# Two graph layers on one core: three dense chunks instead of four, list work at other places, dense R gathered straight to its place

## Chip, cores and metric

The kernel runs on one core of a Trainium2 chip. The metric is the device time in microseconds (us), the median of several runs. Where the profile is read, times are those of one profiled execution.

## What is computed

There are 8 batches of 2048 nodes with 128 features, x[b, n, f], and one matrix adj (2048 x 2048) with about 9 non-zero entries in a row. All data are float32. Layer 0 and layer 1, in short:

```python
sj, si = x @ g_w[:128], x @ g_w[128:256]
res = si[:, :, None] + sj[:, None, :] + adj[None] * g_w[256] + g_b
agg = jnp.einsum('bij,bjd->bid', res, x)
x = layernorm(x + agg @ weight + bias)

x1 = jnp.einsum('bnf,nw->bwf', x, adj)               # hop, order 1
x2 = 2 * jnp.einsum('bnf,nw->bwf', x1, adj) - x      # hop, order 2
xs = concat([x, x1, x2, x1, x2])                     # the same adj twice
x = layernorm(x + relu(xs @ Theta1 + bias1))
```

In layer 0 the product with adj is sparse, and what remains of `res` has low rank: for each half of the batch it is a product of five columns (four of si and one of ones) with five rows (column sums, and the row of sums weighted by sj and g_b with the bias). Both halves together are the "rank-9 part". In layer 1 the five thetas are merged to three: u = x1 th0, y = A'u + x1 th1 (hop 1) and out = layernorm(x1 + relu(A'y + x1 th2 + b)) (hop 2), A' the transposed adj.

## The kernel before

**Tiles.** The nodes are 16 chunks of 128 rows. A row of a chunk holds all 8 batches, 1024 numbers (4 KB), so a chunk's tile is 128 x 1024 (512 KB) and its product fills two PSUM banks. All matmuls are float32.

**Phase A** (loop over R_ORDER, line 328) loads adj row chunk by row chunk (1 MB each), transposes it on PE (row_groups, 244; ACT copies it out and scales it by wr) and stores the transposed columns of most chunks to DRAM (store_rt, 264), where rr_d[c] later holds, for each node, the entries of both directions. SP issues these loads and stores in the order of the list `todo` (pump, 216). Every second step takes a tile of x with it: transposes (x_t, 267) and y0 = x @ weight (y_of, 277). DVE takes block maxima (mask_rows, mask_columns): which rows of 32 columns have a non-zero entry.

**Phase B** (the X loop, 688) does the other eight tiles of x, with the dense product of chunks 0 and 1 (full_rows, 311) after each, and building steps of the lists between (lists_at, 667).

**Lists.** Chunks 4 to 15 do not multiply with all of adj. For each chunk there are seven lists of up to 128 rows: four T lists (32 columns each), two H lists of 64 columns and one of 128 columns. DVE finds the rows with rounds of eight largest numbers (round_of, 463; rounds2, 658), and lists_end (468) turns them into indices (idx, idr). For each list a job gathers the entries of adj from rr_d into staging (get_job, 533, four buffers `st`), and DVE copies them, masked, to `rct` for layer 0 and `rc` for layer 1 (keep_job, 546). Then for each list and each of the three products a gather fetches 128 rows of y0, u or y from DRAM (get_rows, 714), and PE multiplies them (listed, 722). A gather is an indirect DMA that POOL issues, one instruction for a list. Twelve tiles of Y take gathered rows in turn.

**Dense chunks** 0 to 3 are full products in layer 0 only, of 16 blocks x 2 halves of 128 x 512; chunks 2 and 3 run after phase B (777 to 836), between the list jobs. In layer 1 they use lists as well; their entries are gathered from adj into a tile `trp` (28 gathers of 128 x 128) and kept by DVE in `rc`.

**List loop** (839 to 862), chunks 4 to 15 in layer 0: rows and jobs, own block (own_rows, 765), rank9 (614), which needs a small transpose (si_t, 607), the lists, z_add, make_u (647), layernorm (628). x for the sum is loaded by load_z (213) two chunks ahead into ring tiles; own rows of y0 for chunks from 8 on and the own block of adj come by load_own (755) on SP.

**Hops** (865 to 929, called at 931 and 937): for each chunk theta rows (8 matmuls), own rows, T lists, H lists, and `end`. Hop 1 stores y, hop 2 adds x1, takes the layernorm of the chunk and stores 512 KB of output from ACT's queue. The order of chunks is 4 to 13, 0 to 3, 14, 15 in hop 1, and 9 to 13, 0 to 3, 14, 15, 4 to 8 in hop 2; T lists only use rows of the first 14 chunks, so they can start before the last chunks are done.

**What sets the order.** A wrapper (Tied, 66 to 72) keeps each engine's instructions in the order in which the program issues them, in the places near the change. Therefore almost all instructions carry line 72 in the profile, and are told apart by their tiles. Numbers in names of buffers are left out there: `Y<-y_d` stands for gathers from y0_d in layer 0 and from y_d in hop 2. A gather on POOL that waits holds every gather behind it.

Of the kernel before, what the change touches and what calls it, by code (L numbers as in the profile page):

```python
# [18 lines left out]
def kernel(  # L19
# [30 lines left out]
    ND = 4  # L50
# [5 lines left out]
    PAD = 40000  # L56
    W = 3 * P
    T_ORDER = list(range(6, NC)) + [4, 5]
# [3 lines left out]
    X_ORDER = list(range(ND, NC)) + list(range(ND))  # L62
# [27 lines left out]
    rct = keep.tile([P, NS * W], F32, name="rct")  # L90
# [24 lines left out]
    def load_constants():  # L115
        with nc.allow_non_contiguous_dma(reason="two columns of 128 numbers"):
            act.dma_start(out=wx[:, D:D + 2], in_=g_w[0:2 * D].rearrange("(t p) -> p t", p=P))
        act.dma_start(out=wx[:, 0:D], in_=weight)
        act.dma_start(out=wr, in_=g_w[2 * D:2 * D + 1][None, :].to_broadcast([P, 1]))
        act.dma_start(out=gb, in_=g_b[None, :].to_broadcast([P, 1]))  # L120
        for i in range(4):
            act.dma_start(out=b0row[:, i, :], in_=bias0[None, :])
        act.dma_start(out=b1bc[:, 0, :], in_=bias1[None, :].to_broadcast([P, D]))
        act.dma_start(out=th, in_=theta.rearrange("(m p) f -> p m f", p=P))

    ctx.enter_context(nc.allow_non_contiguous_dma(reason="512-byte rows of a block of 128 columns"))
    load_constants()
# [4 lines left out]
    e5 = const.tile([1, 5], F32)  # L132
    dve.memset(e5, 0.0)
    dve.memset(e5[:, 4:5], 1.0)
# [4 lines left out]
    sel5 = const.tile([P, 4, 5], F32)  # L139
    dve.memset(sel5, 0.0)  # L140
    for i in range(4):
        dve.tensor_copy(sel5[:, i, i:i + 1], sel[:, 0:1])
        dve.tensor_copy(sel5[:, i, 4:5], sel[:, 1 + i:2 + i])
# [3 lines left out]
    dve.tensor_copy(num, numi)  # L147
    coli = const.tile([P, NI], I32)
    pool.iota(coli[:, 0:NT], pattern=[[1, NC], [0, QT]], base=0, channel_multiplier=0)
    pool.iota(coli[:, NT:NT + 2 * NC], pattern=[[1, NC], [0, 2]], base=0, channel_multiplier=0)  # L150
# [12 lines left out]
    si = const.tile([P, NC, 37], F32)  # L163
    dve.memset(si, 0.0)
    for h in range(2):
        dve.memset(si[:, :, 32 * h + 4:32 * h + 5], 1.0)
# [16 lines left out]
    ats += [Y[:, n:n + 2].rearrange("p c b f -> p (c b f)") for n in X_ORDER[NX::2]]  # L183

    def at_of(c):
        t = at4[:, c] if c < ND else ats[(c - ND) % len(ats)]
        return t.rearrange("p (j i) -> p j i", i=P)
# [13 lines left out]
    todo += [("x", 8), ("s", 12), ("x", 9), ("s", 13), ("x", 10), ("x", 11), ("s", 14), ("x", 12)]  # L201
    todo += [("s", 15), ("x", 13), ("x", 14), ("x", 15)] + [("c", c) for c in T_ORDER]
# [10 lines left out]
    def load_z(c):  # L213
        zs[c] = load_x(c, [ring[:, 3], ring[:, 4], ring[:, 5], spare][(c - 2) % 4])

    def pump():
        while todo:
            what, n = todo[0]
            if what == "a" and n < done["a"] + 3:
                sp.dma_start(out=am[n % 3], in_=adj[R_ORDER[n] * P:(R_ORDER[n] + 1) * P, :])  # L220
            elif what == "x" and n < done["x"] + 6:
                c = X_ORDER[n]
                xin[c] = load_x(c, ring[:, X_SLOT[n % 6]])
                if c < ND:
                    zs[c] = xin[c]
            elif what == "s" and done["a"] == NC:
                store_rt(n)
            elif what == "c" and done["a"] == NC:
                copies([n])
            else:  # L230
                return
            todo.pop(0)
# [52 lines left out]
    def s_rows(c0):  # L285
# [5 lines left out]
        for h in range(2):  # L291
            act.copy(si[:, c4, 32 * h:32 * h + 4], sraw[:, c4, h * HB:(h + 1) * HB, 1])
# [15 lines left out]
    LAST = list(range(ND)) + list(range(8, NC)) + list(range(4, 8))  # L308
# [18 lines left out]
    pump()  # L327
    for k, n in enumerate(R_ORDER):
# [139 lines left out]
    def lists_end(part):  # L468
# [17 lines left out]
        s = slice(lo, hi)  # L486
        rown = small.tile([P, NT], F32, name=f"rown{part}", tag="rown")[:, 0:hi - lo]
# [4 lines left out]
        dve.scalar_tensor_tensor(rown, rown, float(NC), col[:, s], op0=ALU.mult, op1=ALU.add)  # L492
# [14 lines left out]
    adj128 = adj.rearrange("n (c f) -> (n c) f", f=P)  # L507
# [15 lines left out]

    jobs = [("T", c) for c in T_ORDER] + [("H", c) for c in range(ND, NC)]
    for c in range(ND):
        jobs += [("T", c), ("H", c)]
    got, kept = [0], [0]
    last = trp[:, 2].rearrange("p i f -> p (i f)")

    def staged(k):  # L530
        return st[:, k % 4 * BD:] if jobs[k][1] >= ND else last

    def get_job():
# [3 lines left out]
        for n, i in enumerate(columns(c, what)):  # L537
            if c >= ND:
                gather(
                    s[:, n * 2 * P:(n + 1) * 2 * P], rr_d[c - ND].rearrange("n m f -> n (m f)"), idx,  # L540
                    i, N,
                )
            else:
                gather(s[:, n * P:(n + 1) * P], adj128, idr, i, N * NC)

    def keep_job():
# [3 lines left out]
        m = 2 if c >= ND else 1  # L550
        hc = has[:, columns(c, what)[0]:columns(c, what)[0] + QT]
        for k in range(m):
            if m == 1 or k == 1:
                to = rc[:, c * W:(c + 1) * W]
            else:
                to = rct[:, (c - ND) * W:(c - ND + 1) * W]
            of = s[:, k * P:]
            if what == "T":
                if m == 2:
                    dve.tensor_mul(  # L560
                        to[:, 0:P].rearrange("p (t f) -> p t f", t=QT),
                        strided(of, QT, m * P + TW, TW), hc[:, :, None].to_broadcast([P, QT, TW]),
                    )
                    continue
                for t in range(QT):
                    at = t * (P + TW)
                    dve.tensor_scalar(
                        to[:, TW * t:TW * t + TW], of[:, at:at + TW], hc[:, t:t + 1], None,
                        op0=ALU.mult,
                    )  # L570
                continue
            step = m * P + 64
            dve.tensor_mul(
                to[:, P:2 * P].rearrange("p (t f) -> p t f", t=2), strided(of, 2, step, 64),
                hc[:, 0:2, None].to_broadcast([P, 2, 64]),
            )
            i = NT + 2 * NC + c
            dve.tensor_scalar(
                to[:, 2 * P:3 * P], of[:, 2 * m * P:2 * m * P + P], has[:, i:i + 1], None,
                op0=ALU.mult,  # L580
            )

    def make_ub():
# [4 lines left out]
        for h in range(2):  # L588
            pe.matmul(
                pu[32 * h:32 * h + 5], e5, b0row.rearrange("p i f -> p (i f)"), start=True,  # L590
                stop=False, skip_group_check=True, tile_position=(0, 32 * h),
            )
        for i in range(4):
            s = slice(i * P, (i + 1) * P)
            for h in range(2):
                pe.matmul(
                    pu[32 * h:32 * h + 5, s], sel5[:, i, :], cs[h][:, s], start=False, stop=(i == 3),
# [9 lines left out]
    def si_t(c):  # L607
        b = bank[turns[turn[0] % len(turns)]][0:37, 0:P]
        turn[0] += 1
        pe.transpose(b, si[:, c, :], ident)  # L610
        sits[c] = small.tile([37, P], F32, name=f"sit{c}", tag="sit")
        act.copy(sits[c], b)

    def rank9(c, accs):
        sit = sits.pop(c)
        for h in range(2):
            pe.matmul(
                accs[h], sit[32 * h:32 * h + 5], ub[32 * h:32 * h + 5].rearrange("p i f -> p (i f)"),
                start=False, stop=(c < ND), skip_group_check=True, tile_position=(32 * h, 0),
# [47 lines left out]
    def lists_at(n):  # L667
        if n == 9:
            ranked()
        if n == 10:  # L670
# [3 lines left out]
            dve.tensor_reduce(miss[:, 1:2], both, AX.XY, ALU.add)  # L674
            thetas()
        if n == 13:
# [3 lines left out]
            encode2()  # L680
            get_job()
            get_job()
        if n == 14:
            split2()
        if n == 15:
            candidates2()

    for n in range(NX, NC):
        xt = x_t(n)
        pump()  # L690
        y_of(n, xt)
        lists_at(n)
        for c, acc in enumerate((acc0, acc1)):
            full_rows(c, acc, [X_ORDER[n - 1]])
# [12 lines left out]
    load_z(4)  # L707

    NG = 12
    G = [flat(Y[:, n]) for n in LAST[:NG]]  # L710
    g_at = [0]
    rows_of = {}

    def get_rows(i, c, what, src):
        hi = LT if what == "T" else NC
        for n, q in enumerate(columns(c, what)):
            g = G[g_at[0] % NG]
            g_at[0] += 1
# [3 lines left out]
    def listed(i, c, accs, what):  # L722

        r = rc[:, c * W:(c + 1) * W] if i else rct[:, (c - ND) * W:(c - ND + 1) * W]
# [26 lines left out]
    homes = [seven[(c + 8) % 12 % 7] for c in range(12)] + [slab(k) for k in range(4)]  # L751
# [21 lines left out]
    def own0(c):  # L773
        load_own(0, y0_d, c, Y[:, c] if c < 8 else ring[:, c % 2], c < 8)


    rounds2([0])
# [3 lines left out]
    rounds2([1, 2])  # L781
# [4 lines left out]
    load_z(ND + 1)  # L786
    rounds2([3, 4])
# [4 lines left out]
    rank9(1, acc1)  # L792
    rounds2([5, 6])
    next_job()
    rounds2([7])
    lists_end(1)
# [4 lines left out]

    acc2 = bank[4:6]
    full_rows(2, acc2, LAST[:5])
    next_job()
    next_job()
    make_u(0, zs[0], x1t[0], u_of[0], 0)
    layernorm(zs[1], "0_1")
    full_rows(2, acc2, LAST[5:11])
    next_job()
    make_u(1, zs[1], x1t[1], u_of[1], 0)  # L810
    next_job()
    full_rows(2, acc2, LAST[11:])
    si_t(2)
    rank9(2, acc2)
    z_add(acc2, zs[2])
    overflow()
    next_job()
    layernorm(zs[2], "0_2")

    acc3 = bank[2:4]  # L820
    full_rows(3, acc3, LAST[:8])
    next_job()
    next_job()
    get_rows(0, ND, "T", y0_d)
    get_rows(0, ND, "H", y0_d)
    own0(ND)
    own0(ND + 1)
    full_rows(3, acc3, LAST[8:])
    keep_job()
    keep_job()  # L830
    get_rows(0, ND + 1, "T", y0_d)
    si_t(3)
    rank9(3, acc3)
    si_t(ND)
    z_add(acc3, zs[3])
    layernorm(zs[3], "0_3")


    for c in range(ND, NC):
        if c > ND:  # L840
            if c > ND + 1:
                get_rows(0, c, "T", y0_d)
            get_rows(0, c, "H", y0_d)
        if c < 15:
            keep_job()
        if c < 13 or c == 14:
            get_job()
        accs = acc_pair()
        own_rows(0, c, accs, True)
        if c + 2 < NC:  # L850
            own0(c + 2)
        rank9(c, accs)
        if c + 1 < NC:
            si_t(c + 1)
        listed(0, c, accs, "T")
        listed(0, c, accs, "H")
        z_add(accs, zs[c])
# [177 lines left out]
```

## Time and profile before

| | us |
|---|---|
| median of 3 runs (lowest, highest) | 810.49 (807.04, 811.39) |
| the profiled execution | 818.08 |
| its span | 816.3 |
| PE matmul busy | 732.8 (90%), 3554 instructions |
| DVE busy | 394.7 (48%) |
| POOL busy | 445.2 (55%), 432 instructions |
| ACT busy | 192.7 (24%) |
| DMA | 253.90 MB, mean 311 GB/s |
| mean granted clock | 0.971 of full speed |

Busy time is that of the engine's records; POOL's are mostly gathers, and a record of a gather is its issue on POOL, not the transfer. "Idle before" names what ended a wait; "issue" is time in which the engine waited for nothing that the profile shows. DMA share is the busy share of the core's 16 DMA engines.

The chain of work that ended last is 52% PE, 29% DMA and 6% issue. By transfer, 12% is `Y<-u_d` (gathers in hop 1) and 8% `Y<-y_d`.

### The profile page before, as it was taken

Reading aid. Unit: us, or ns where it says so; the run is one execution under the profiler, and the core shown is the slowest. Engines: PE = TensorE matmul, PEld = TensorE weight load, DVE = VectorE, ACT = ScalarE, POOL = GpSimd, SP = SyncE. Lnnn points to the kernel's source line nnn. Section 1 sums busy time; section 2 is a strip of 40 time slices with the busy share of each in tenths; the row PEclk is TensorE's granted clock in tenths of the full one; section 3 lists DMA queues with packets and bytes.
Section 4 is the critical chain, followed back from the end, with each engine's and each line's share of the span. In section 5 each row is a group of like instructions: output and inputs, shape, how many; then the busy total and the mean of one; then the engine's idle time right before and its main releaser. Section 6 shows DMA issues by size and latency. Waiting matters only on the chain.

```text
span 816.3 us, 10067 instructions
## 1 busy us (share of the span) xinstructions
PE 732.8 (90%) x3554; PEld 364.9 (45%) x3554; DVE 394.7 (48%) x591; ACT 192.7 (24%) x439; POOL 445.2 (55%) x432
## 2 busy tenths in 40 slices
PE   4999999997999998988798888898899999999992
PEld 4666566642644343434345243333344454444441
DVE  4664876578341655555533000000100377777775
ACT  3757554321200332313222000000000011111101
POOL 1000000477747876776344677776774777776740
PEclk9999999997999999999899899999999999999997
DMA  8999999999326799999969799899999799999982
GB/s 264 296 314 316 352 292 295 314 398 347 119 89 223 244 346 368 341 344 367 356 224 344 246 364 360 314 365 346 339 372 357 252 343 357 370 385 389 363 299 68
DMA packets 165299, 253.90 MB, mean 311 GB/s; under 512 B 17255, under 2 KB 118020, under 8 KB 163192
## 3 DMA queue, kind: packets, MB, share of 16 engines
q0 software_dynamic: 49280, 146.52, 49.7%
q1 hardware_dynamic: 93200, 81.01, 31.1%
q10 hardware_dynamic: 22760, 25.63, 8.9%
q8 instruction: 30, 0.49, 0.2%
q14 instruction: 29, 0.24, 0.1%
HBM read 234.82 MB, written 58.72 MB: 360 GB/s over the span
## 4 chain that ended last, share of the span: by engine, by line
PE 52%; DMA 29%; issue 6%; ACT 6%; DVE 3%; POOL 2%; ACTq 0%; POOLq 0%; SPq 0%; DVEq 0%
PE bank L72 52%; DMA Y<-u_d,idx 12%; DMA Y<-y_d,idx 8%; DMA st<-rr_d,idx 2%; DMA rd<-rr_d 2%; ACT Y L72 2%; DMA ring<-in_x_dram 2%; POOL Y L72 1%; ACT rct L72 1%; ACT trp L72 1%; DMA trp<-in_adj_dram,idr 1%; DVE s L72 1%; DVE ring L72 1%; ACT at L72 1%; DVE st L72 1%
## 5 line engine op out<-in xcount | busy, mean ns | idle before, releaser
L72 POOL DMA_INDIRECT Y<-y_d,idx x196 | 212.0, 1081 | 93.2 <-PE bank L72 38.0
L72 PE MATMUL bank<-Y,rc 128*32 128x512 f32 (+2 forms) x896 | 219.7, 618 | 21.3 <-DMA Y<-u_d,idx 19.1
L72 POOL DMA_INDIRECT st<-rr_d,idx x84 | 90.3, 1075 | 183.5 <-DVE rown L72 148.3
L72 POOL DMA_INDIRECT Y<-u_d,idx x112 | 111.8, 999 | 53.9 <-issue 29.9
L72 PEld LDWEIGHTS bank<-Y,rc 128*32 128x32 f32 (+2 forms) x896 | 58.6, 130 | 179.3 <-issue 99.5
L72 PE MATMUL bank<-Y,at 128*128 128x512 f32 x256 | 115.2, 601 | 0.0
L72 PE MATMUL bank<-Y,rct 128*32 128x512 f32 (+2 forms) x336 | 77.3, 625 | 8.5 <-DMA Y<-y_d,idx 8.5
L72 DVE TENSOR_REDUCE s<-sq 128x4 f32<-128x512 f32 x64 | 43.9, 686 | 58.0 <-ACT sq L72 58.0
L72 PEld LDWEIGHTS bank<-Y,at 128*128 128x128 f32 x256 | 47.8, 193 | 53.6 <-issue 53.4
L72 DVE COPY ring<-bank 128x512 f32<-128x512 f32 x10 | 6.9, 692 | 110.1 <-PE bank L72 110.1
L72 ACT ACTIVATE sq<-ring 128x512 f32<-128x512 f32 x44 | 27.7, 630 | 129.5 <-DVE ring L72 109.7
L72 PE MATMUL bank<-ring,rd 128*128 128x512 f32 x108 | 51.5, 599 | 5.7 <-DMA rd<-rr_d 4.1
L72 PE MATMUL bank<-ident,rc 128*128 128x128 f32 (+2 forms) x302 | 45.0, 297 | 12.6 <-DMA rc<-in_adj_dram 6.6
L72 PE MATMUL bank<-th,at 128*128 128x128 f32 x384 | 49.2, 283 | 1.9 <-ACT at L72 1.9
L72 PEld LDWEIGHTS bank<-th,at 128*128 128x128 f32 x384 | 46.8, 197 | 6.7 <-ACT at L72 3.8
L72 DVE TENSOR_TENSOR ring<-bank,ring 128x512 f32<-128x512 f32 x26 | 17.3, 688 | 66.0 <-PE bank L72 60.8
L72 DVE TENSOR_REDUCE st<-rc 128x64 f32<-128x2048 f32 x16 | 36.5, 2283 | 25.7 <-DMA rc<-in_adj_dram 25.7
L72 ACT COPY ring<-bank 128x512 f32<-128x512 f32 x34 | 19.9, 586 | 122.5 <-PE bank L72 112.9
L72 PEld LDWEIGHTS bank<-Y,rct 128*32 128x32 f32 (+2 forms) x336 | 20.8, 130 | 57.3 <-issue 32.4
L72 PEld LDWEIGHTS bank<-ident,rc 128*128 128x128 f32 (+2 forms) x302 | 33.8, 150 | 25.5 <-issue 9.1
L72 PE MATMUL bank<-wx,trp 128*128 128x130 f32 x256 | 36.9, 288 | 4.3 <-ACT trp L72 2.2
L72 PE MATMUL bank<-ident,ring 128*128 128x128 f32 x232 | 32.5, 282 | 6.4 <-DMA ring<-in_x_dram 2.8
(142 smaller groups left out, 789.1 us busy)
## 6 DMA issues: line engine op xcount, KB each, us to landing
rc<-in_adj_dram SPq DMA_DIRECT2D x16, 1024.0 KB, 10.9
ring<-in_x_dram SPq DMA_DIRECT2D x25, 512.0 KB, 8.5
rr_d<-in_adj_dram SPq DMA_DIRECT2D x12, 1024.0 KB, 10.8
rr_d<-Y SPq DMA_DIRECT2D x8, 1024.0 KB, 9.0
y_d<-Y SPq DMA_DIRECT2D x16, 512.0 KB, 10.6
u_d<-ring ACTq DMA_DIRECT2D x12, 512.0 KB, 7.0
ring<-y_d SPq DMA_DIRECT2D x11, 512.0 KB, 23.2
ring<-u_d SPq DMA_DIRECT2D x10, 512.0 KB, 3.9
```

What stands on the lines that cost most here:

```text
L72: return lambda *a, **k: tc.keep_in_program_order(f(*a, **k))
```

## The change

1. ND is 3: chunk 3 is no longer dense. It has lists, a stored transpose (store_rt) and a column copy like chunks 4 to 15. Its entries for layer 0 lie in a corner of `at4`.
2. Steps of lists_at run at three places in a step of x: ahead of y_of, after it, and between the two dense chunks' matmuls. The candidates, lists_end(0), the first four jobs, split2 and candidates2 come at earlier places, and the first three rounds of the second lists run within the x loop.
3. Entries of chunks 0 to 2 for layer 1 are gathered straight into `rc` by 21 indirect DMAs of 128 x 32, 64 or 128 (get_direct), after POOL has set that part of rc to zero. The 28 gathers into trp and their keeps are gone. 17 of the 21 are issued in the list loop, four in hop 1.
4. For list chunks the rank-9 part becomes nine rows in the third H list: rows 119 to 127 of its row tile hold u (ub_rows writes them once into two fixed tiles, C0), and si is written into the entries of the same rows (si_rows, 13 small matmuls). rank9 and si_t remain for the dense chunks. Each H job has one more DVE operation on rows 96 to 127, an addition.
5. Gathered rows use different tiles: in layer 0 ten in turn (seven of Y, ring 0 and 1, Y 3) and two (C0) for the third H list; in the hops twelve of Y. Own rows of y0 stay in Y for chunks 3 to 11. z is loaded into x1t[c], up to four chunks ahead.
6. At the start, adj rows come in two loads of 512 KB, wr is the first constant, and six later constants move to SP's list behind the 16 adj chunks and the first tiles of x.
7. Hop 1 begins three chunks (T lists, theta and own rows) before its loop instead of two, the third in banks 4 and 5, and its order starts at chunk 3. In hop 2 the last two chunks are computed by halves of the batch: by_halves does the matmuls of one half, then its sum, layernorm and a 256 KB store, the end of a half being issued after the beginning of the next.

The core of the diff (constants, tables for rank 9 and indices of columns left out):

```diff
-    ND = 4
+    ND = 3
...
-    ats += [Y[:, n:n + 2].rearrange("p c b f -> p (c b f)") for n in X_ORDER[NX::2]]
+    ats += [at4[:, 3]] + [Y[:, n:n + 2].rearrange("p c b f -> p (c b f)") for n in X_ORDER[NX::2]]
...
     def load_z(c):
-        zs[c] = load_x(c, [ring[:, 3], ring[:, 4], ring[:, 5], spare][(c - 2) % 4])
+        zs[c] = load_x(c, x1t[c])
...
-                sp.dma_start(out=am[n % 3], in_=adj[R_ORDER[n] * P:(R_ORDER[n] + 1) * P, :])
+                for w in (slice(0, N // 2), slice(N // 2, N)):
+                    sp.dma_start(
+                        out=am[n % 3][:, w], in_=adj[R_ORDER[n] * P:(R_ORDER[n] + 1) * P, w]
+                    )
...
+    def get_direct(n):
+        for at, w, i in direct[:n]:
+            gather(
+                rc[:, at:at + w], adj.rearrange("n (c f) -> (n c) f", f=w), idr, i, N * (N // w)
+            )
+        del direct[:n]
...
+    def si_rows(c0, n):
+
+        b = by4(bank[turns[turn[0] % len(turns)]])[LC:]
+        turn[0] += 1
+        for i in range(n):
+            pe.matmul(
+                b[:, i, :], si[:, c0 + i, :], ident, start=True, stop=True, skip_group_check=True,
+                tile_position=(0, LC),
+            )
...
     for n in range(NX, NC):
         xt = x_t(n)
         pump()
+        lists_at(n, 0)
         y_of(n, xt)
-        lists_at(n)
-        for c, acc in enumerate((acc0, acc1)):
-            full_rows(c, acc, [X_ORDER[n - 1]])
+        lists_at(n, 1)
+        full_rows(0, acc0, [X_ORDER[n - 1]])
+        lists_at(n, 2)
+        full_rows(1, acc1, [X_ORDER[n - 1]])
+        if n == 14:
+            rounds2([0])
+        if n == 15:
+            rounds2([1, 2])
...
-    NG = 12
-    G = [flat(Y[:, n]) for n in LAST[:NG]]
-    g_at = [0]
+
+
+    G0 = [flat(Y[:, n]) for n in LAST[:7]] + [flat(ring[:, 0]), flat(ring[:, 1]), flat(Y[:, 3])]
+    C0 = [flat(ring[:, 5]), flat(spare)]
+    G1 = [flat(Y[:, n]) for n in list(range(4)) + list(range(8, NC))]
...
     for c in range(ND, NC):
-        if c > ND:
-            if c > ND + 1:
-                get_rows(0, c, "T", y0_d)
+        if c > 4:
+            get_rows(0, c, "T", y0_d)
+        if c > 3:
             get_rows(0, c, "H", y0_d)
-        if c < 15:
-            keep_job()
-        if c < 13 or c == 14:
-            get_job()
-        accs = acc_pair()
-        own_rows(0, c, accs, True)
+        k, g = (2, 2) if c < 5 else (2 if c in (7, 8) else 1 if c < 15 else 0, 1 if c < 13 else 0)
+        for n in range(max(k, g)):
+            if n < k:
+                keep_job()
+            if n < g:
+                get_job()
+        get_direct(0 if c < 8 else 1 if c < 13 else 3)
+        if c == 3:
+            accs = acc3
+        else:
+            accs = acc_pair()
+            own_rows(0, c, accs, True)
         if c + 2 < NC:
             own0(c + 2)
-        rank9(c, accs)
-        if c + 1 < NC:
-            si_t(c + 1)
         listed(0, c, accs, "T")
         listed(0, c, accs, "H")
...
         for k, c in enumerate(order):
+            if i == 2 and k >= NC - 2:
+                rows(k, "H")
+                rows(k + 1 if k + 1 < NC else NC, "T")
+                by_halves(k)
+                continue
             rows(k, "H")
-            if k > 1:
+            if k >= begun:
                 begin(k)
-            fetch(k + 2)
-            if k > 0:
+            if k + 2 >= begun:
+                fetch(k + 2)
+            if k + 1 >= begun:
                 rows(k + 1, "T")
-            if i == 1 and (k % 2 and k < 12 or k == 12):
-                keep_job()
-                if k < 12:
-                    get_job()
+            if i == 1:
+                get_direct(1)
             listed(i, c, accs[k], "H")
             end(c, accs[k])
```

In by_halves, a half of a chunk runs as follows (its matmuls, from the transposes to list H, write one bank only):

```python
                zh, sq = begun_half(homes[c], accs[h], b, h, s)
                if halves:
                    ended_half(*halves.pop())
                halves.append((c, zh, sq, h, s))
            if k == NC - 1:
                ended_half(*halves.pop())
```

## The prediction, made before the result was known

> **What bounds the kernel now.** I read the span in stretches first: one row a stretch, with its length, the busy time of PE, PEld, DVE, ACT and POOL (instructions in brackets), the clock, the DMA share and GB/s.
>
> ```profile
> 0.00:109.50 109.50, 91.22 (x504) 63.23 (x505) 69.03 (x60) 64.10 (x145) 2.82 (x12) 1.00 0.98 307
> 109.50:173.90 64.40, 61.59 (x325) 39.81 (x326) 42.21 (x75) 26.66 (x97) 17.33 (x17) 1.00 1.05 316
> 173.90:262.10 88.20, 80.49 (x288) 36.47 (x288) 43.09 (x85) 13.72 (x26) 62.04 (x59) 0.92 0.62 213
> 262.10:429.50 167.40, 149.76 (x734) 67.05 (x735) 91.29 (x153) 47.79 (x96) 108.50 (x106) 0.98 0.92 324
> 429.50:451.70 22.20, 16.81 (x121) 10.86 (x119) 6.11 (x8) 6.06 (x11) 11.01 (x11) 0.99 0.91 326
> 451.70:625.20 173.50, 158.70 (x697) 63.94 (x698) 13.87 (x35) 9.38 (x16) 125.52 (x127) 0.95 0.95 345
> 625.20:641.40 16.20, 14.35 (x81) 6.43 (x79) 0.69 (x1) 0.00 (x0) 6.26 (x7) 1.00 0.64 228
> 641.40:801.40 160.00, 159.90 (x817) 77.12 (x816) 121.00 (x167) 23.41 (x45) 111.70 (x98) 1.00 0.96 344
> 801.40:816.30 14.90, 0.00 (x0) 0.00 (x0) 7.39 (x10) 1.56 (x3) 0.00 (x0) 0.66 0.24 73
> ```
>
> I call them A (adj turned), B (rest of x), C (dense chunks), D (list chunks of layer 0), E (turn), F (hop 1), G (turn), H (hop 2), I (tail). PE is busy 90% and looks like the bound. It is in C and H. In A and B the DMA engines are full. POOL's 55% hides the rest: its timeline (start, length, idle before it) shows that a gather busy for 1.0 us is always followed by 0.3 us that no wait explains.
>
> ```profile
> 223.66 1.00 POOL L72 DMA_INDIRECT st<-rr_d,idx  x1 [0.30 <-issue]
> 224.96 0.99 POOL L72 DMA_INDIRECT st<-rr_d,idx  x1 [0.30 <-issue]
> 234.74 1.00 POOL L72 DMA_INDIRECT st<-rr_d,idx  x1 [8.79 <-DVE rc L72]
> 399.08 0.99 POOL L72 DMA_INDIRECT Y<-y_d,idx  x1 [0.30 <-issue]
> 410.68 0.99 POOL L72 DMA_INDIRECT Y<-y_d,idx  x1 [10.61 <-PE bank L72]
> ```
>
> So a gather costs 1.30 us of POOL. With its small stretches I measure, start to start, 1.36 over the 55 from 151.7 to 225.0 and 1.365 over the 129 from 447.4 to 622.2. That last run is stage F: 129 x 1.365 = 176 us. F is POOL's queue, and the DMA engines (0.95) are close behind. In D the pitch is 1.33 to 1.42, plus stalls of 8.8, 4.5 and 10.6 us; the one at 399 is PE late, because a transfer of own entries (rd) took 19.4 us. The groups of POOL in F give the mean length of each kind:
>
> ```profile
> L72 POOL DMA_INDIRECT Y<-u_d,idx x99 | 98.0, 990 | 35.3 <-issue 21.2 <-PE bank L72 8.0 <-DMA Y<-u_d,idx 6.0
> L72 POOL DMA_INDIRECT trp<-in_adj_dram,idr x20 | 20.0, 999 | 9.4 <-issue 4.9 <-DVE rc L72 3.3 <-DMA Y<-u_d,idx 1.3
> ```
>
> A gather of 64 KB (trp) costs POOL what one of 512 KB (Y) does. Last, two stretches in which DMA is the limit, 371 to 394 GB/s:
>
> ```profile
> 590.00:622.00 32.00, 30.65 (x148) 13.08 (x149) 2.08 (x3) 1.76 (x3) 23.16 (x24) 0.95 1.00 380
> 720.00:740.00 20.00, 20.00 (x105) 9.73 (x104) 15.90 (x22) 2.97 (x6) 15.53 (x15) 1.00 1.03 394
> ```
>
> **The change part by part.**
>
> *A and B.* The first x tile now is not behind late constants: PE waited for it until 16.5, and I take 4.5 us off (2.5 to 6.5). But DMA is full (share 1.05), and chunk 3 by lists adds a 1 MB store (3.2 us at 316 GB/s) and a column copy (3.45 us each in SP's rows). Sixteen more load issues and six constants pass SP in A, where SP waits for room anyway: nothing, or +1 if a load is late. The stores of y0, queued behind it all on SP, landed at 193; I take 195 (191 to 198). The row gathers wait for them. The list steps moved between pairs of x bring the first lists some 7 us earlier (lists_end(0) at 150 before) and the second's rounds (DVE, 167.6 to 191.2) some 11. Those DVE steps were beside full DMA and PE; what could show is PE behind them in its queue, +0 to 2.
>
> *C and D.* Off PE: dense chunk 3, 27.6 us (the trace has two records of 0.43 for each of 16 x 2 matmuls), and rank9 with si_t, 1.06 + 0.23 for 12 chunks, 15.5. On PE: a listed chunk, 7.4 with its own rows, the few ub_rows and si_rows, about 4. Off DVE: the 24 keep operations of dense chunks, most of them in F. On DVE: one more small operation (0.28) for each H job, hidden, as DVE is busy 91 of 167 in D. PE thus loses 32 us in C and D, if PE bounded them.
>
> POOL does not lose. Its order in the new program has 32 gathers of adj entries before the first row gather of layer 0. From that one to the last row gather of layer 0 stand 91 row gathers, 59 of entries, 11 straight to rc: 161, and one memset of 128x1152. No row of before has this memset; from its DVE likes (0.51 for 128x512) I bound it between 0.6 and 3 and take 2. The straight gathers have no row either: 128x32 to 128x128, nearest trp with 1.30; below (0, if the queue has room) and above (2.6, if small rows take twice as long) I take 1.30. Here a rule speaks against the change: the Trainium skill (DMA: Bandwidth & Descriptors, Bandwidth) asks for transfers of 1 MiB, its table giving 0.95 us of DMA for 64 KB and 6.15 for 1 MB, so that small ones are nearly pure overhead. By the rule 21 gathers for 28 with a quarter or half of the bytes gains only on bytes. By the trp row the count is what POOL pays, 7 x 1.30 = 9 us less. I follow the row.
>
> Before, the same stretch began at 239.6 (the first Y gather) after a run of 58 entries. After: 195 + 161 x 1.35 + 2 = 414, with landing (8.0 median) and the last lists on PE (5) 427, against 429.5: -2. By the ends of the pitch (1.30, 1.42) and stalls of 0 to 8 us the last gather is at 406 to 434: D ends between -10 and +17, the far end needing both. The three stalls of before (24 us) go: own rows stay in Y for chunks 4 to 11 (four loads of 0.5 MB fewer on SP), z loads run four ahead, and dense staging is gone. But 14 gathers of chunk 3 (18 us) and 11 straight ones (14 us) take the room. So what PE saves is not seen; next late are Y rows.
>
> *E.* The chain make_u, store of u, first gather is unchanged; six straight gathers (7.8 us) hide in its wait, where four stood. 0.
>
> *F.* POOL issues 111 instead of 129 gathers here (16 fewer small ones, and two more rows of u before the stage), hence 111 x 1.365 = 152 us. PE needs 9.13 a step, 146. DMA: 59.9 MB in the stage, less 20 small gathers (1.0), two T lists moved ahead of it (0.9) and own rows (0.5), is 57.4 MB. The same page gives an HBM limit of 358 GB/s for a core: 160 us. The two stretches above ran at 380 and 394: 146 to 151. Both measured above the figure, but not throughout; taking 365 I get 157 us: -16 (-10 to -22).
>
> *G and H.* H is PE at 159.9 of 160; nothing goes there. Halves of the last two chunks add short DVE operations: +0 to 2, I take 0.
>
> *I.* Only half a chunk is left after PE: 0.68+0.69+0.69+0.17+0.69, ACT 0.63, DVE 0.69, ACT 0.3, 0.2+0.69 = 5.5, and a 256 KB store for 512 (about 4.7 with the end): 10.2 for 14.9, -4.7 (-3 to -5.5).
>
> Sum: -2 + 0 - 16 + 0 - 4.7 = -23. Span 816.3 gives 793.5; the profiled execution is 1.8 longer (818.08), 795.3. It lay 7.6 above the median of 810.49, so the forecast on the median's scale is 788.
>
> **The rivals.**
>
> *Layer 0 profits too* (0.13): POOL keeps 1.30, stalls stay away. Last gather 195 + 211 = 406, D ends 10 earlier rather than 2, and A's 4.5 also arrive: about 775. For it: most rows show 0.30 idle. Against: each run of over 50 gathers averaged 1.36 or more.
>
> *DMA takes hop 1's gain* (0.15): at 345 GB/s as now, 57.4 MB need 166 us, -7: 797. For it: share 0.95 already. Against: 380 at the end of F, when POOL ran on.
>
> *Slower: POOL in layer 0* (0.12). Gathers of chunk 3 and the straight ones go in one queue with rows, and wait for buffers: now ten for rows, and two hold list H's last, where twelve stood. If waits bring the pitch to 1.60, the last gather is at 455, D ends 38 later, and with F and I the median is 828. It is slower from D +21, that is a last gather at 437 and a pitch of 1.50. For it: 24 us of stalls in the trace. Against: PE, which frees the buffers, has 32 us less to do.
>
> *It does nothing* (0.05): F is DMA's, D slips by 6 to 10: 806 to 812.
>
> **How the numbers follow.** The likeliest (0.55) is 788, with D's ends, F's and the tail's: 774 to 800. To take in 8 of 10, the range reaches to 771 and 808. A measurement of this kernel can tell 0.5% (806.4 to 814.5) from no change. Faster 0.81, same 0.07, slower 0.12.
>
> **What would show it.** POOL: first row gather near 195, the last of layer 0 near 414, no stall over 5 us; F about 157 us with some 111 gathers and over 360 GB/s; the tail 10 us from PE's last matmul. PE would be idle in D (under 130 busy of a longer stretch). It would be wrong if gathers from 195 to 414 average 1.5 or more, if y0's stores land after 205, or if hop 1's steps stay at 11 us.

## The result, and the profile after

The changed kernel is slower: 820.7 us (median of 6 runs, 819.21 to 824.44) against 810.96 (6 runs, 807.04 to 817.85), a ratio of 1.0117 (95% interval 1.0069 to 1.0166). The forecast was 788 and its range ended at 808. The profiled execution took 819.62 us, its span is 817.8.

The profile of before that the prediction was made on was not a typical execution: 818.08 us, 7 above the median. A second profile of the same kernel (run g0 below) took 811.52 (span 809.7). The two profiles of the changed kernel (the one here and run f0 below) lie within 3 us of each other up to the end of hop 1. So the changed kernel is set beside the second profile of before here. First the stretches of the second profile of before, then those of the changed kernel, cut at the same events: first row gather of layer 0, end of the last list chunk on PE (D ends), first H gather of hop 1 (E ends), first H gather of hop 2 (F and G end), PE's end (H), end. The columns are those of the prediction's first table.

```profile
238.57:422.55 183.98, 170.27 (x788) 76.29 (x787) 95.43 (x168) 48.20 (x98) 127.95 (x120) 1.00 0.89 316
422.55:443.37 20.82, 17.99 (x121) 11.07 (x118) 6.11 (x8) 6.05 (x11) 8.48 (x10) 1.00 0.95 343
443.37:627.25 183.88, 164.92 (x750) 68.83 (x751) 14.58 (x36) 9.36 (x16) 128.89 (x130) 0.98 0.93 341
627.25:794.80 167.55, 164.43 (x843) 77.90 (x841) 120.84 (x166) 23.40 (x45) 114.30 (x104) 0.99 0.94 337
794.80:809.70 14.90, 0.01 (x1) 0.00 (x0) 7.39 (x10) 1.56 (x3) 0.00 (x0) 0.62 0.25 73
```

```profile
200.80:433.50 232.70, 187.89 (x812) 82.37 (x811) 120.91 (x218) 56.64 (x104) 178.52 (x169) 0.95 0.83 273
433.50:459.75 26.25, 22.89 (x139) 13.65 (x138) 6.16 (x8) 6.06 (x11) 12.46 (x13) 1.00 0.96 374
459.75:632.47 172.72, 161.38 (x732) 67.60 (x731) 11.06 (x16) 9.36 (x16) 109.74 (x112) 0.98 0.95 351
632.47:805.24 172.77, 168.23 (x843) 77.80 (x841) 123.56 (x175) 24.11 (x47) 119.43 (x104) 1.00 0.91 328
805.24:817.80 12.56, 0.00 (x0) 0.00 (x0) 6.05 (x12) 1.12 (x3) 0.00 (x0) 0.59 0.22 67
```

Read off the ends: D at 422.6 before and 433.5 after (+10.9), then E +5.4, F -11.2, H +5.2, I -2.3; the sum is the +8.1 between the two spans. Hop 1 did win, 11.2 us of the forecast 16; three other stages ate it. PE lost the dense chunk and the rank-9 products, yet its busy time from the start to the end of D fell by 12.5 us (380.6 in g0, 368.1), not by 32; it may be that the matmuls of a list, whose rows now come one by one, run apart where they ran side by side. In D it is busy 188 of 233 us and idle for 45, and 38 of these it waits for gathered rows. The waits of PE in D (total, times, longest), first in g0, then in the changed kernel:

```profile
PE bank L72 <- DMA Y<-y_d,idx: 6.9, 10, 1.3
```

```profile
PE bank L73 <- DMA Y<-y_d,idx: 25.8, 14, 11.8
PE bank L73 <- DMA ring<-y_d,idx: 6.1, 4, 3.1
PE bank L73 <- DMA trp<-y_d,idx: 6.1, 3, 4.6
```

So what PE saved was worth nothing in D.

POOL's timeline of the changed kernel shows the places. A row has start, length and, in brackets, the idle time before it with what ended it.

```profile
186.08 1.00 POOL L73 DMA_INDIRECT st<-rr_d,idx  x1 [0.30 <-issue]
200.80 0.99 POOL L73 DMA_INDIRECT Y<-y_d,idx  x1 [13.72 <-DMA rd<-rr_d]
...
430.35 1.24 POOL L73 DMA_INDIRECT rc<-in_adj_dram,idr  x1 [0.30 <-issue]
432.93 0.99 POOL L73 DMA_INDIRECT Y<-u_d,idx  x1 [1.34 <-PE bank L73]
...
448.96 1.00 POOL L73 DMA_INDIRECT rc<-in_adj_dram,idr  x1 [0.64 <-DMA Y<-u_d,idx]
459.75 0.99 POOL L73 DMA_INDIRECT Y<-u_d,idx  x1 [9.80 <-issue]
...
791.29 1.18 POOL L73 DMA_INDIRECT Y<-y_d,idx  x1 [6.43 <-PE bank L73]
```

At 186 POOL has issued the 32 gathers of entries and stands for 13.7 us until y0 is stored (the releaser named is a transfer queued right behind the stores). From there to the last row gather of layer 0, at 422.54, it issues 161 gathers with no stall over 2.6 us: 221.7 us less 1 for the memset, 1.37 each (divided by 161, as the prediction counts). Then six small gathers, and the first gather of u is at 432.9 (420.8 before). At 450 it waits 9.8 us, as it seems for the last store of u (this profile names nothing, but those of g0 and f3 name `u_d<-st` at this place), and at 785 6.4 us for PE. The chain of the page says the same: 44% PE instead of 52, 34% DMA instead of 29.

One correction to what stands ahead of the prediction: the gathers on POOL do not come in the program's order in the trace; it looks as if they were placed where their buffers and inputs are ready. The program has 14 of the 21 small gathers in the list loop and seven in hop 1; in the trace 17 come before the first gather of u. That is how six small gathers stand right ahead of the gathers of u, three of them out of hop 1.

### The profile page after: what moved, and what is told of

It reads as the page before. It is cut to its first block, busy times and chain, and to the rows that moved or that the text cites. A ratio compares the mean times of both kernels' runs of the same rounds, so it can differ in the third digit from the quotient of the medians.

```text
span 817.8 us, 10050 instructions
## 1 busy us (share of the span) xinstructions
PE 720.6 (88%) x3496; PEld 355.7 (43%) x3496; DVE 401.7 (49%) x611; ACT 195.1 (24%) x439; POOL 455.2 (56%) x440
## 4 chain that ended last, share of the span: by engine, by line
PE 44%; DMA 34%; issue 7%; ACT 6%; DVE 3%; POOL 3%; POOLq 0%; SPq 0%; ACTq 0%; DVEq 0%
PE bank L73 44%; DMA Y<-u_d,idx 16%; DMA Y<-y_d,idx 9%; DMA trp<-y_d,idx 4%; ACT Y L73 2%; DMA ring<-in_x_dram 2%; POOL Y L73 2%; DMA st<-rr_d,idx 2%; DMA ring<-y_d,idx 1%; ACT trp L73 1%; ACT at L73 1%; DVE s L73 1%; ACT rct L73 1%; POOL st L73 1%; DMA wr<-in_L_gnn_g_w_dram 1%
## 5 line engine op out<-in xcount | busy, mean ns | idle before, releaser
L73 POOL DMA_INDIRECT Y<-y_d,idx x175 | 193.2, 1104 | 87.2 <-issue 29.0
L73 PE MATMUL bank<-Y,at 128*128 128x512 f32 (+2 forms) x216 | 90.2, 596 | 0.0
L73 PE MATMUL bank<-Y,rct 128*32 128x512 f32 (+1 forms) x228 | 65.8, 625 | 26.9 <-DMA Y<-y_d,idx 25.8
L73 PEld LDWEIGHTS bank<-Y,at 128*128 128x128 f32 (+2 forms) x216 | 35.9, 183 | 39.0 <-issue 38.1
L73 ACT COPY ring<-bank 128x512 f32<-128x512 f32 (+1 forms) x36 | 21.0, 585 | 119.2 <-PE bank L73 119.2
L73 ACT ACTIVATE sq<-ring 128x512 f32<-128x512 f32 x26 | 16.4, 630 | 122.9 <-DVE ring L73 91.2
L73 PE MATMUL bank<-ring,rd 128*128 128x512 f32 x96 | 45.3, 593 | 0.0
L73 PEld LDWEIGHTS bank<-Y,rct 128*32 128x32 f32 (+1 forms) x228 | 13.6, 121 | 72.9 <-issue 34.7
L73 PE MATMUL bank<-ring,rct 128*32 128x512 f32 (+2 forms) x84 | 38.1, 632 | 6.8 <-DMA ring<-y_d,idx 6.1
L73 ACT COPY Y<-bank 128x256 f32<-128x256 f32 (+1 forms) x72 | 27.8, 397 | 41.6 <-PE bank L73 41.4
## 6 DMA issues: line engine op xcount, KB each, us to landing
y_d<-Y SPq DMA_DIRECT2D x16, 512.0 KB, 10.3
```

Source lines behind the costliest of these rows:

```text
L73: return lambda *a, **k: tc.keep_in_program_order(f(*a, **k))
```

## Experiments

Every ratio is to the kernel before on the same chip in the same session. Chips differ: on some the kernel before takes 810 us, on others 851 to 856.

**First set: three undone parts, and before again.** Edits to the changed kernel. e2 takes the halves of hop 2 out:

```diff
-            if i == 2 and k >= NC - 2:
+            if i == 2 and k >= NC:
```

e3 puts make_u of chunk 15 first at the turn:

```diff
+        between()
         begin(0)
         if i == 1:
             fetch(2)
             rows(2, "T")
-        between()
         begin(1)
```

e4 moves 12 small gathers from layer 0 to hop 1 and holds them there behind row gathers:

```diff
-        get_direct(0 if c < 8 else 1 if c < 13 else 3)
+        get_direct(0 if c < 8 else 1 if c < 13 else 0)
...
-                get_direct(1)
+                with tc.issue_after(last_gather[0].ins):
+                    get_direct(2)
```

> The kernel before, unchanged, for a second profile, because its first profile lay 7 us above its median. If the late transfer of own entries at 382 and the 10.6 us stall of POOL behind it were an accident of that execution, list chunks of layer 0 end about 7 to 10 us earlier here and the execution is near 811. If they belong to the kernel, it is again near 818 in the profile and stage by stage the same.

> The changed kernel, but hop 2 ends with whole chunks as before. Theory (computing by halves holds row buffers until the second half, so the last two gathers wait 6.4 us for PE and PE waits for them): hop 2 takes 168 us instead of 172.8 and the tail 14.9 instead of 12.6, together 2 us faster than the changed kernel. Rival (halves save the 4.7 us that the forecast gave them, and hop 2 is longer for another reason): 2 to 5 us slower than the changed kernel.

> The changed kernel, but at the turn to hop 1 make_u of chunk 15 comes before the first chunk's theta rows, own rows and T lists on PE. Theory (PE waits in order for the T rows of u, which POOL issues late, and make_u of 15 stands behind that wait): make_u of 15 starts near 441 instead of 448, hop 1's first H gather 7 us earlier, the whole 5 to 8 us faster than the changed kernel. Rival (the store of u is late because the DMA engines are busy with twelve T gathers): within 2 us of the changed kernel.

> The changed kernel, but 12 of the 17 small gathers straight into rc that POOL issued in layer 0 come in hop 1, behind its row gathers. Theory (layer 0 and the turn are POOL's queue, hop 1 is the DMA engines' with room on POOL): the last row gather of layer 0 comes 8 us earlier, the first of u 16 us earlier, and hop 1 takes the 12 for nothing to 5 us more: 8 to 14 us faster than the changed kernel. Rival (hop 1 is POOL's queue as well): 12 x 1.3 us come back there and nothing is gained, within 2 us.

All four ran on a chip where the kernel before takes 851 us (27 runs). Before again was 0.998 (0.995 to 1.001) of it, e2 1.035, e3 1.032, e4 1.047. The changed kernel itself was not among them, so nothing can be said of the edits; the set is inconclusive. What it shows is that on this chip all three versions of the changed kernel lose 3 to 5%, where the changed kernel lost 1.2 on the first.

**Second set: the control and single edits.** The control is the changed kernel; f1 and f2 are e3 and e4 again. f3 moves the stores of y0 ahead:

```diff
-    todo += [("s", 12), ("x", 13), ("x", 14), ("x", 15)] + [("c", c) for c in range(ND, NC)]
+    todo += [("s", 12), ("x", 13), ("x", 14), ("x", 15)] + [("c", c) for c in range(ND, 11)]
...
-    for n in range(NC):
+    for n in X_ORDER:
         sp.dma_start(out=y0_d[n * P:(n + 1) * P, :], in_=flat(Y[:, n]))
+    copies(range(11, NC))
```

> The changed kernel again, unchanged, as the control for the other three on the same chip. Theory and rival alike: its time stands to the kernel before as in the first result (1.007 to 1.017), if the chip is like the first one.

> The changed kernel with make_u of chunk 15 ahead of the first chunk's T lists at the turn to hop 1, beside the changed kernel on the same chip. Theory (make_u stands behind a wait for T rows): 5 to 8 us faster than the control, the first H gather of hop 1 that much nearer to the last row gather of layer 0. Rival (the DMA engines are late with u): within 2 us.

> The changed kernel with 12 of the 17 small gathers moved from layer 0 behind row gathers of hop 1, beside the control. Theory (POOL's queue sets layer 0, not hop 1): 8 to 14 us faster than the control. Rival (hop 1 is POOL's queue too): within 2 us.

> The changed kernel with five of the thirteen column copies on SP moved behind the stores of y0, and these in the order in which x is done. Theory (the row gathers start late because the stores of y0 stand behind 48 us of copies): the first row gather comes near 188 instead of 201, the POOL wait of 13.7 us before it goes, and layer 0 ends 8 to 13 us earlier. Rival (in layer 0 the end is set by PE and transfers, not by when POOL's row gathers begin): within 3 us.

Measured (median; ratio to before, 809.97): control 824.95 (1.0167, 1.0118 to 1.0215); f1 819.53 (1.0112, 1.0073 to 1.0151); f2 825.12 (1.0177, 1.0137 to 1.0218); f3 817.44 (1.0079, 1.0054 to 1.0104).

The median of f1 is 5.4 us below the control's, the size that the theory gave, but the two intervals overlap, and the first result's ratio for the changed kernel was 1.0117: as a gain in time this is not shown. The change at the turn is to be seen in PE's timeline; first the changed kernel, then f1. `bank<-Y,rc` are T lists of u, `ident,rct` the transposes of make_u of chunk 15.

```profile
440.81 1.04 PE L73 MATMUL bank<-Y,rc 128*32 128x512 f32 x2 [0.65 <-DMA Y<-u_d,idx]
442.85 1.05 PE L73 MATMUL bank<-Y,rc 128*32 128x512 f32 x2 [0.99 <-DMA Y<-u_d,idx]
444.58 1.04 PE L73 MATMUL bank<-Y,rc 128*32 128x512 f32 x2 [0.69 <-DMA Y<-u_d,idx]
446.18 1.90 PE L73 MATMUL bank<-Y,rc 128*32 128x512 f32 x10 [0.55 <-DMA Y<-u_d,idx]
448.01 1.09 PE L73 MATMUL bank<-ident,rct 128*128 128x128 f32 x8
```

```profile
439.77 2.05 PE L73 MATMUL bank<-th,rct 128*128 128x128 f32 x16 [0.24 <-ACT rct L73]
447.50 1.97 PE L73 MATMUL bank<-ident,rct 128*128 128x128 f32 x8 [5.68 <-DVE rct L73]
```

In the changed kernel the transposes stand behind T lists whose rows come one by one from POOL. In f1 they only wait for DVE's layernorm. (Layer 0 ended 5 us later in f1's profile than in the control's, so the start of make_u is the same there; from the first gather of u to the first H gather it is 24.0 us instead of the control's 29.0; it was 26.8 in the first profile of the changed kernel.)

f2 gains nothing, and its rival was right. Layer 0's last row gather came 4.7 us earlier than in the control (417.4 for 422.1), but POOL then stood 10.9 us (the profile names PE) at the place where the six small gathers had been, and hop 1, with 124 instead of 111 gathers up to the first H gather of hop 2, took 179.3 us instead of 172.8. So hop 1 has not the room that the theory gave it: 13 gathers more took 6.5 us more, 0.5 each. And the six ahead of u had cost next to nothing.

f3 is 7.5 us faster, and its interval is clear of the control's. SP's queue of the changed kernel and of f3:

```profile
121.74 48.52 SPq L73 DMA_DIRECT2D rr_d<-in_adj_dram  x13
170.36 24.09 SPq L73 DMA_DIRECT2D y_d<-Y  x16
```

```profile
124.47 26.55 SPq L73 DMA_DIRECT2D rr_d<-in_adj_dram  x8
151.07 25.20 SPq L73 DMA_DIRECT2D y_d<-Y  x16
176.32 20.99 SPq L73 DMA_DIRECT2D rr_d<-in_adj_dram  x5
```

The stores start 19 us earlier, but the first row gather only 5.3 (196.0 for 201.3), since it then waits 6.9 us for PE to free its tile. The theory had asked for 188 and for an end of layer 0 that is 8 to 13 us earlier. In the profiles the last row gather of layer 0 comes 2.1 us earlier and PE's last list chunk ends 4.0 earlier; how the median's 7.5 divides over the stages, one profile cannot show.

**Third set: chunk 3 dense again, and mends together.** g2 is the changed kernel with ND = 4: full_rows(3) as before, 12 list chunks, 28 small gathers, 14 of them in hop 1, held there behind row gathers. g3 is f1, f3 and e2 in one; g5 is these three mends in g2.

> The kernel before once more, for a profile near its median on a chip like the first. If the late own entries and the 10.6 us stall of POOL were an accident of the first profile, the first H gather of hop 1 comes near 440 instead of 447 and the execution is near 811; if they belong to the kernel, it is again 447.

> The changed kernel with chunk 3 dense again (four dense chunks, 12 by lists, 28 small gathers straight into rc, 14 of them in hop 1). Against the changed kernel POOL has 14 gathers of chunk 3 fewer and 7 small ones more, SP one copy and one store fewer, and PE 27.6 us of dense work for 7.4 of lists. Theory (from the first list to the end of hop 1 time goes by the number of gathers on POOL): 7 x 1.36 and 4 us from the copy are gained, 9 to 13 us faster than the changed kernel, near the kernel before. Rival (PE sets layer 0): 10 to 20 us slower than the changed kernel.

> The changed kernel with three mends: stores of y0 ahead of five copies, make_u of chunk 15 first at the turn, hop 2 without halves. Theory (each gave 7.5, 5.4 and, by the profile, 2 us): 12 to 15 us faster than the changed kernel, 0.995 to 1.003 of the kernel before. Rival (two of them release the same wait): 7 us faster only, 1.006.

> The three mends and chunk 3 dense again. Theory (the gains are of different waits and add): 20 to 25 us faster than the changed kernel, 0.985 to 0.992 of the kernel before. Rival (with layer 0's row gathers early and fewer, PE with dense chunk 3 becomes the bound): no faster than the three mends alone.

Ratios to before (810.57, 59 runs): g0 1.0013 (0.9992 to 1.0034), g2 1.0101 (1.0068 to 1.0133), g3 1.0014 (0.9994 to 1.0033), g5 1.0026 (1.0005 to 1.0048). In g0 the 10.6 us stall in the list loop is gone, and so it is in e1's profile: it belonged to the first execution. The first H gather of hop 1 comes at 443.4 instead of 447.4, so 4 of the 7 us that D ends earlier are left there.

The three mends bring the changed kernel back to the level of before. That is 1.5% below the control's ratio, as the sum of the theory asked, but only 1.0% below the first result's, and neither ran in this set; that the gains add in full is not shown. g2 lies 0.2 to 0.7% below the changed kernel's two ratios, less than the theory's 9 to 13 us, far from the rival's loss. Its profile shows both halves of that: layer 0's last row gather at 411.8 (422.1 in the control), 10 us won; hop 1 183.8 us for 172.8, with eleven more small gathers in it, 11 us lost. And POOL stands 10.3 us, to 259.6, for PE, which does dense chunk 3 to 253 and then chunk 4's first lists. So g5, too, is no faster than g3.

**Fourth set: number or place.** h1 is g5 with the 28 small gathers elsewhere: 8 early in the list work, 8 after the last row gather of layer 0, 6 after the T gathers of u, 6 in hop 1. h4 is h1 with the last chunk of hop 2 alone by halves. h2 and h3 are edits of the kernel before: h2 leaves the rank-9 part of chunks 4 to 15 out of the sum, h3 has 14 gathers more:

```diff
-        rank9(c, accs)
-        if c + 1 < NC:
-            si_t(c + 1)
```

```diff
+        with tc.issue_after(last_gather[0].ins):
+            for n in [c - ND] if c < 14 else [10, 12] if c == 14 else [11, 13]:
+                gather(more[:, n % 8, :], adj32, idr, n, N * NC)
```

> The kernel with chunk 3 dense and three mends (it ran at 1.0026 of the kernel before), with its 28 small gathers at other places: 8 early in the list work, where POOL waits later for dense chunk 3, 8 behind the last row gather of layer 0, 6 behind the T gathers of u, 6 in hop 1. Theory (a small gather costs 1.3 us where POOL's queue is the bound and nothing inside a wait that it has anyway): 6 to 12 us faster than that kernel, 0.989 to 0.996 of the kernel before. Rival (a small gather costs about the same everywhere): within 2 us of 1.0026.

> The kernel before without rank9 and si_t in its list loop (the rank-9 part of chunks 4 to 15 is left out of the sum), so PE has 15 us less to do in layer 0. Theory (POOL's queue bounds the list loop): 0 to 3 us faster than the kernel before, 0.996 to 1.000. Rival (PE, 90% busy there, is the bound): 10 to 15 us faster, 0.982 to 0.988.

> The kernel before with 14 small gathers more in its list loop (128 x 32 entries of adj into a tile that nothing reads), one or two for each chunk. Theory (each gather costs a pitch of 1.3 us of POOL's queue, and little wait is left there): 10 to 18 us slower than the kernel before, 1.012 to 1.022. Rival (small gathers go beside other work): 0 to 4 us slower.

> h1_placed, with only the last chunk of hop 2 by halves. Theory (halves of chunk 14 hold buffers for which the last two gathers wait; those of the last chunk hold nothing that anyone waits for): 2 to 3 us faster than h1_placed, PE's end not later and the tail 12.6 instead of 15 us. Rival (halves lengthen PE's work as such): within 1 us of it or slower.

These ran on a chip where before takes 855.7 us (21 runs). h3 was 1.0226 (1.0165 to 1.0287), 19 us (14 to 25): 14 x 1.3 is 18. Its groups on POOL in layer 0 have the small gathers at the length of the large ones:

```profile
L72 POOL DMA_INDIRECT Y<-y_d,idx x84 | 90.1, 1072 | 41.8 <-issue 19.9 <-PE bank L72 16.5 <-remote 4.8
...
L72 POOL DMA_INDIRECT more<-in_adj_dram,idr x14 | 14.0, 1000 | 4.3 <-issue 4.3
```

h2, with 15 us less of PE's work, was not faster: 1.0084 (1.0050 to 1.0118). Why it was even slower stays open. That PE's rank-9 work does not bound the list loop of the kernel before is likely by this, but not shown: in h2's profile ACT stood 20.5 us in the list loop with nothing named and POOL 10.0 us for DVE, and such stalls (last section) can hide what PE saved. h1 was 1.0164 (1.0076 to 1.0252) and h4 1.0191 (1.0114 to 1.0268) here, while the kernel that they were to beat had run on another kind of chip. So both were run again:

> h1_placed again, on another chip. Theory as there: a small gather costs nothing inside a wait that POOL has anyway; on a chip where the kernel before takes about 811 us, 0.989 to 0.996 of it. Rival (the same cost everywhere): 1.000 to 1.005.

> h4_placed_last_half again: 2 to 3 us faster than i1_placed by the theory (only halves of chunk 14 hold buffers that someone waits for), within 1 us or slower by the rival.

Before took 810.21 (11 runs); i1 took 800.52, 0.9885 (0.9848 to 0.9922), and i2 799.92, 0.9869 (0.9832 to 0.9906). Both beat the kernel before and the changed kernel. What i1 has of the change are parts 2 to 6 and the third chunk begun early of part 7; chunk 3 is dense, and there are no halves. POOL's timeline at the turn, first g0, then i1:

```profile
420.82 1.00 POOL L72 DMA_INDIRECT Y<-u_d,idx  x1 [10.68 <-DMA rd<-in_adj_dram]
...
443.37 0.99 POOL L72 DMA_INDIRECT Y<-u_d,idx  x1 [8.19 <-DMA u_d<-st]
```

```profile
403.27 0.99 POOL L73 DMA_INDIRECT trp<-y_d,idx  x1 [0.30 <-issue]
404.56 1.00 POOL L73 DMA_INDIRECT rc<-in_adj_dram,idr  x1 [0.30 <-issue]
...
413.71 1.00 POOL L73 DMA_INDIRECT rc<-in_adj_dram,idr  x1 [0.30 <-issue]
415.38 1.89 POOL L73 DMA_INDIRECT Y<-u_d,idx  x1 [0.67 <-issue]
...
438.52 1.00 POOL L73 DMA_INDIRECT rc<-in_adj_dram,idr  x1 [0.30 <-issue]
440.62 0.99 POOL L73 DMA_INDIRECT Y<-u_d,idx  x1 [1.11 <-DMA Y<-u_d,idx]
```

Eight small gathers fill the wait for u's rows and six the wait for its last store; both waits, 10.7 and 8.2 us in g0, are down to about 1. Beside g5, which differs from i1 only in these places, the last row gather of layer 0 is at 403.3 (410.8), hop 1 takes 175.1 us (181.0), and the turn between, with eleven more small gathers in it, 37.3 (33.2). So a gather's place decides what it costs: at the turn about 0.4 us.

i2 is within 1 us of i1, as its rival said. The last stretch of PE, first i1, then i2, shows what halves cost of their own:

```profile
774.90 6.44 PE L73 MATMUL bank<-Y,rc 128*32 128x512 f32 x28
781.18 1.04 PE L73 MATMUL bank<-ident,Y 128*128 128x128 f32 x8
```

```profile
781.86 1.12 PE L73 MATMUL bank<-Y,rc 128*128 128x512 f32 x2 [0.39 <-DMA Y<-y_d,idx]
782.83 0.60 PE L73 MATMUL bank<-ident,Y 128*128 128x128 f32 x4
783.26 1.06 PE L73 MATMUL bank<-th,Y 128*128 128x128 f32 x8
784.15 1.02 PE L73 MATMUL bank<-st,rd 128*128 128x512 f32 x2
785.11 3.13 PE L73 MATMUL bank<-Y,rc 128*32 128x512 f32 x14
```

A chunk as a whole does theta, own rows and T lists of both halves while its last rows are on the way. By halves, all of the second half's work, 5.4 us, follows the landing of the last rows (781.9). i2's PE ends 3 us later after the first H gather of hop 2 than i1's, and its tail is 2.1 us shorter (12.4 for 14.5).

## Why the prediction was wrong, step by step

**A and B, "I take 195".** The first row gather came at 200.8. The sum gave the stores of y0 a further 3.2 us for a store and 3.45 for a copy, less 4.5 that the start gains. On SP the gain went to the added store: the copies began at 121.7 as before. Then 13 of them at 3.73 us stood where there had been 12 at 3.51 (3.67 in g0), 3 us more than the one copy that was counted, so the stores started 6.4 us later (170.4 for 163.9) although PE was 2.5 us ahead; and SP's row of the stores took 24.1 us for 21.6. f3 shows that this order of copies and stores cost 7.5 us. SP's queue was named, but only the added copy was priced.

**C and D, "-2": the step that failed.** It put POOL's stretch at 195 to 414 and set this against a stage end of 429.5. The mechanism was right for the changed kernel: POOL issues without a stall over 2.6 us while PE waits 38 us for rows, and g2, with 27.7 us of dense chunk given back to PE and 14 gathers fewer from the first row gather to the last, has the last one 10 us earlier (4 of them by an earlier start). h3 says the same of the kernel before. Three sizes were off. The start, 5.8 us. The pitch, 1.37 for 1.35, 3 us. And the base, 7 us: 429.5 was the end of an execution with a 10.6 us stall of its own; in g0 it is 422.6. Against that the forecast's own 427 was already a loss of 4, not a gain of 2. (The memset took 1 us for 2, and landing and last lists 11 for 13; with these the sum comes to the 12.9 us between -2 and +10.9.) I had seen that the profile lay 7.6 us over the median and carried this as a constant through the sum, when the larger part of it belonged to the very stage whose stalls I let the change remove. One of these stalls was misread besides: the one of 8.8 us ended at 234.7, ahead of the first row gather at 239.6, so 15 us of stalls lay in D, not 24.

**E, "0".** It was 26.3 us for 20.8 (+5.4). That six small gathers hide in a wait was right (f2: moving them away gains nothing). Missed was that a third set of T gathers and late POOL put a wait into PE's order ahead of make_u of chunk 15; with two lines exchanged (f1) the stretch from the first gather of u to the first H gather was 3 to 5 us shorter. "The chain is unchanged" was true of the data and false of the queue.

**F, "-16".** -11 against g0, -13 against the first profile. The stage ran at 351 GB/s, where I took 365, below two short stretches (380, 394) that do not tell the rate of a whole stage. The 358 GB/s that the prediction took from the Trainium skill (DMA: Bandwidth & Descriptors, Bandwidth) would have come nearer: by it, an estimate, the 60.6 MB between the two H gathers (172.7 us at 351) need 169 us. But the page gives it for two cores that stream from one HBM domain, and more for one core alone, so that it fits here may be luck; no run varied it.

**H, "0 to 2", and I, "-4.7".** H +5.2 and I -2.3. In the changed kernel the last two gathers are held up 6.4 us by PE, for tiles that the second half of the last chunk but one still reads, and after they land a half's work is still to do. In the tail the DVE order puts the end of the half before (reduction, wait for ACT's root, reciprocal, product: 808.42 to 810.9) between the last half's subtraction and its own reduction: 2.4 us that the sum of the last half alone did not have. g3, without halves, had PE's end 168.2 us after the first H gather of hop 2 instead of 172.8, and the end 183.3 instead of 185.3.

**The rivals.** The slower one named POOL in layer 0 and asked for a last gather at 437 and a pitch of 1.50; the pitch stayed at 1.37, so the loss did not come by its mechanism. It came from shortfalls of 2 to 13 us in five stages: D 12.9, E 5.4, F 4.8, H 5.2, I 2.4, together 30.7 of the 32.7 us between 788 and 820.7; the rest is how the profiles lie to the medians. Part 3's small gathers were right at 1.30 by the trp row (17 of them up to the end of D at 1011 ns and 0.3); the page's table of DMA time by size does not tell what POOL pays to issue one.

## What to carry to other kernels

Where one engine's queue bounds a stage, count its instructions and place them: a gather cost 1.3 us in the list loop (h3), 0.5 to 1.0 in hop 1 (f2, g2) and 0 to 0.4 inside a wait that the queue has anyway (f2, i1). Placing the same 28 gathers accordingly was worth 1.4%, about 11 us (i1 against g5). Before summing against a profile, look which stage holds its distance from the median. When work is split to shorten a tail, ask what it had been doing while the last transfer was on its way, and who waits for the buffers that the second half still reads.

## What the runs showed of the hardware that was not expected

On the chips where the kernel before takes 851 to 856 us, engines stand still with nothing that the profile names: on PE 45.2 us in all in the list e1 gives for its waits.

```profile
PE bank L72 <- issue: 45.2, 41, 8.5
```

Columns: total, times, longest. ACT's longest such wait there was 25 us (h2), and the changed kernel's versions suffered more than the kernel before. Their granted clock was lower too (0.91 to 0.94 in e2 to e4, 0.95 to 0.97 in the kernel before on that chip); whether as a cause or because PE stood still, no run tells. What the engines wait for stays open; no run varied it. A kernel's gain on one chip (0.9885 for i1) was a loss on another (1.0164 for the same kernel as h1).
